# Spreading B with one bf16 product of three parts instead of an fp32 product, in a kernel whose scans run on VectorE

## The chip, the cores and the metric

The kernel runs on one core of a Trainium2 chip. Its time is the device time of one launch in microseconds (us). Before the change the median of three runs is 10359.18 us (10338.47 to 10376.03).

A core has a matrix engine (TensorE, "PE" in the profile, with its weight loads as "PEld"), VectorE ("DVE"), ScalarE ("ACT") and GpSimd ("POOL"). Each works through its own queue in order, and semaphores order the engines among themselves. The queue "SP" only issues DMAs here.

## The reference

The input is x of shape (4, 56, 56, 96), four images of 3136 tokens with 96 channels. Layers 0 and 1 are state-space layers with 192 inner channels and 16 states, each scanned in four directions; layers 2 and 3 are a linear attention and a quantised feed-forward net each. What matters here is the scan of layers 0 and 1, which is the same for each of the 4 images, 2 layers and 4 directions:

```python
xz = jnp.einsum('bld,kd->blk', seq, xw)
dt_raw = xz[..., :DT_RANK]
b_ssm = xz[..., DT_RANK:DT_RANK + D_STATE]
c_ssm = xz[..., DT_RANK + D_STATE:]
dt = jax.nn.softplus(jnp.einsum('blr,dr->bld', dt_raw, dtw) + dtb)
a = -jnp.exp(A_log)
d_a = jnp.exp(dt[..., None] * a)
d_b = dt[..., None] * b_ssm[:, :, None, :]

def step(h, inp):
    da_t, db_t, x_t, c_t = inp
    h = da_t * h + db_t * x_t[..., None]
    y_t = jnp.einsum('bds,bs->bd', h, c_t)
    return (h, y_t)
```

So for every token there is, per channel and state, a decay exp(dt * a), an input dt * u * B, the recurrence, a product with C, and a sum over the states. dt, B and C are linear in the sequence.

## The kernel before

**Chunks and rounds.** A sequence is cut into 7 chunks of 448 tokens. With 2 layers, 4 images and 4 directions that makes 224 chunks. A chunk has 8 rounds r = 0 to 7: two halves e of the 192 channels times four groups q of states. So there are 1792 rounds. One round holds 128 partitions (4 states times 32 channels) times 3 groups g of 448 tokens.

**What a round does.** In `begin` TensorE spreads B over the partitions: `spread_b` (L560 to L564) multiplies the tile `cf`, which holds C, B and the low-rank part of dt as rows of the chunk, with the 0/1 matrix `sel`, in fp32, into the single PSUM buffer `b`. VectorE multiplies `du` (dt times u, spread by DMA) with `b` into `v` for groups 0 and 1 (L645). Group 2 is made by GpSimd (L625), from a copy of B that came by DMA with C in `cb`; in the rounds listed in `OWN` or `OWN_TAIL` VectorE makes group 2 as well. `OWN_TAIL` holds for images 1 to 3 of layer 1, `OWN` for all others. ScalarE makes the decays `da` in PSUM (L617). VectorE then runs three scans (L670), GpSimd multiplies all three groups with C into `hc` (L680), and two rounds later `add_up` has TensorE sum over states into `y` with four products of 32 columns (L700). ScalarE copies `y` out (L707).

**Zero products.** Ahead of these four products `add_up` issues bf16 products of a zero matrix with `some`, the upper halves of fp32 words, which change nothing in `y` (L696). Their number is fixed when the program is built: as many as the round's other listed work falls short of `WARM`, divided by `FILL`. `self.work` counts what `spend` was told since the last `add_up`, times `PER_P`; neither B's product nor the four sums are in it.

**Preparing the next chunks.** During the 8 rounds of a chunk, `prepare` makes the next one ready: at r = 0 `rows` (ScalarE copies the projection from PSUM into `cf`), at r = 1 `step_sizes` (C and B to memory, first product for dt), at r = 2 `softplus` (ScalarE, with a change of its function table), at r = 3 and 4 `times_u` (GpSimd), then the spreading DMAs. `project_step` (L423) projects the chunk after that at r = 6 and 7, in fp32.

**The order of the work.** In the scans the order on each engine is the order of the program text. Beside the scans run lanes: the rest of the network for other images (norms, convolutions, projections), as generators that are resumed twice a round, at places "C" and "F", under budgets for ScalarE and TensorE. On TensorE the order of one round is: the lanes' products at "C", B's product for the next round, zero products and the four sums of two rounds ago, projections, the lanes' products at "F". A product that waits holds up all that stands behind it. Few lines carry the places that matter:

```python
ps = self.psum.tile([128, 512], F32, tag="b", name="b", bufs=1)[:, :CS]
self.nc.tensor.matmul(ps, self.sel[:, q], ch.cf, start=True, stop=True)
...
for _ in range(int(max(0.0, WARM - self.work) / FILL + 0.5)):
    nc.tensor.matmul(self.y[:C], self.zeros, self.some, start=False, stop=False)
```

After the scans the lanes that remain run alone, until the end.

Of the kernel before, what the change touches and what calls it, by code (L numbers as in the profile page):

```python
# [11 lines left out]
F32 = mybir.dt.float32  # L12
F16 = mybir.dt.float16
BF16 = mybir.dt.bfloat16
F8 = mybir.dt.float8e5
AF = mybir.ActivationFunctionType
ALU = mybir.AluOpType
# [5 lines left out]
C = 96  # L23
DI = 192
NS = 16
NE = 2
NG = 3
NQ = 4
# [4 lines left out]
CS = 448  # L33
# [2 lines left out]
RANK = (12, 6)  # L36
NW, LATE_NW = 13, 20
NWIN = 3
OWN = (3, 4)
OWN_TAIL = (3, 4)  # L40

SPARE = (1.2, 3.0)
# [3 lines left out]
DEPTH, LATE_DEPTH = 3, 6  # L46


WARM, FILL, PER_P = 1.5, 0.19, 0.58

ORDER = (((0, 0), (0, 1), (1, 0), (1, 1)), ((0, 1), (1, 0), (1, 1), (0, 0)))
WD = NE * 64 + NE * C + NE + NE * NQ * NG

# [29 lines left out]
def lay_out(i):  # L85
    i = {k: np.asarray(v) for k, v in i.items()}
    c96, c128, w96, w128, q96, q128 = Cols(C), Cols(128), Cols(C), Cols(128), Cols(C), Cols(128)
    p0, p1 = "L0_conv_", "L1_conv_"

    for n in ("norm_w", "norm_b", "norm2_w", "norm2_b", "ffn_b2"):  # L90
        c96.add("0" + n, i[p0 + n][:, None])
    for n in (
        "dw_b bn1_g bn1_b bn1_m bn1_v pw_b bn2_g bn2_b bn2_m bn2_v ln_g ln_b fus_b fus_ln_g fus_ln_b"
    ).split():
        c96.add("1" + n, i[p1 + n][:, None])
    c96.add("1dw_w", i[p1 + "dw_w"].reshape(C, 9))
    for l in "23":
        c96.add(l + "bq", i[f"L{l}_attn_bqkv"][:C, None])
        c96.add(l + "bff", i[f"L{l}_attn_bff"][:, None])
        c96.add(l + "b2", i[f"L{l}_ffn_b2"][:, None])  # L100
        c128.add(l + "b1", i[f"L{l}_ffn_b1"].reshape(3, 128).T)

    scan = (
        (i[p0 + "ssm_xw"], i[p0 + "ssm_dtw"], i[p0 + "ssm_dtb"], i[p0 + "ssm_Alog"], i[p0 + "ssm_D"]),
        (
            i[p1 + "x_proj_w"],
            i[p1 + "dt_w"],
            i[p1 + "dt_b"],
            i[p1 + "A_logs"].reshape(4, DI, NS),
            i[p1 + "Ds"].reshape(4, DI),  # L110
        ),
    )
    wd = np.zeros((2, 4, 128, WD), np.float32)
    for l, (xw, dw, db, al, dd) in enumerate(scan):
        r = RANK[l]
        for k in range(4):
            t = xw[k].T
            m = np.zeros((128, NE, 64), np.float32)
            m[:C, :, :32] = np.concatenate([t[:, r + NS :], t[:, r : r + NS]], 1).reshape(NE, C, 32).swapaxes(0, 1)
            m[:C, :, 32 : 32 + r] = t[:, :r].reshape(NE, C, r).swapaxes(0, 1)  # L120
            wt = np.zeros((128, DI), np.float32)
            wt[32 : 32 + r] = dw[k].T
            bias = np.zeros((128, NE), np.float32)
            bias[:C] = db[k].reshape(NE, C).T
            a = al[k].reshape(NE, NG, 32, 4, NQ).transpose(3, 2, 0, 4, 1).reshape(128, -1)
            wd[l, k] = np.concatenate([m.reshape(128, -1), wt, bias, a], 1)
        c128.add(f"{l}D", dd.T.reshape(NE, C, 4).swapaxes(0, 1))
    c128.add("0dir", np.broadcast_to(i[p0 + "dir_w"], (128, 4)))
    c128.add("0b1", i[p0 + "ffn_b1"].reshape(3, 128).T)
    for n, v in (  # L130
        ("1conv_b", i[p1 + "conv_b"][:, None]),
        ("1conv_w", i[p1 + "conv_w"].reshape(DI, 9)),
        ("1g", i[p1 + "out_norm_g"][:, None]),
        ("1b", i[p1 + "out_norm_b"][:, None]),
    ):
        c128.add(n + "a", v[:128])
        c128.add(n + "b", v[128:])

    w96.add("0in", _in_blocks(i[p0 + "in_w"].T))
    w96.add("1in", _in_blocks(i[p1 + "in_proj_w"].T))  # L140
    w96.add("0w1", i[p0 + "ffn_w1"].T)
    w96.add("1pw", i[p1 + "pw_w"])
    f = i[p1 + "fus_w"].T
    w96.add("1fa", f[:C])
    w96.add("1fb", f[C:])
    w96.add("1out", i[p1 + "out_proj_w"])
    w = i[p0 + "out_w"].T
    w128.add("0outa", w[:128])
    w128.add("0outb", w[128:])
    w128.add("0w2", i[p0 + "ffn_w2"].T.reshape(3, 128, C).transpose(1, 0, 2))  # L150
    for l in "23":
        w96.add(l + "qkv", i[f"L{l}_attn_Wqkv"])
        w96.add(l + "ff", i[f"L{l}_attn_Wff"])
        q96.add(l + "w1", i[f"L{l}_ffn_W1"].T)
        q128.add(l + "w2", i[f"L{l}_ffn_W2"].T.reshape(3, 128, C).transpose(1, 0, 2))
    bqkv = np.stack([i[f"L{l}_attn_bqkv"] for l in "23"])
    cols = {"c96": c96, "c128": c128, "w96": w96, "w128": w128, "q96": q96, "q128": q128}
    arrays = {"x": np.ascontiguousarray(i["x"]).reshape(NB, L, C), "bqkv": bqkv, "wd": wd}
    arrays.update({k: v.array() for k, v in cols.items()})
    return arrays, {k: v.at for k, v in cols.items()}  # L160


class Net:
# [81 lines left out]
    def setup(self):  # L245
        nc, tc, const = self.nc, self.tc, self.const
        par = self.par
        self.tiles = {}
        for g in ("c96", "c128", "w128"):
            t = const.tile(list(self.aps[g].shape), F32, name=g)  # L250
# [43 lines left out]
        m = const.tile([128, 1], F32, name="wmax")  # L294
# [29 lines left out]
        for n, bias in (("bn1", "1dw_b"), ("bn2", "1pw_b")):  # L324
            s = const.tile([C, 1], F32, name=n + "s")
            t = const.tile([C, 1], F32, name=n + "t")
# [13 lines left out]
        self.b2q = const.tile([C, 2], F32, name="b2q")  # L340
        with tc.tile_pool(name="stage", bufs=1) as st:

            self.sel = const.tile([64, NQ, 128], F32, name="sel")
            for q in range(NQ):
                nc.vector.tensor_copy(
                    self.sel[:, q].rearrange("p (s d) -> p s d", s=4),
                    self.ident[:64, NS + q : NS + q + 13 : 4].unsqueeze(2).to_broadcast([64, 4, 32]),
                )
            self.some = self.upper(self.tiles["w128"][:, :CS])
            self.zeros = const.tile([128, C], BF16, name="zeros")  # L350
# [1 line left out]
            t = st.tile([C, 2, 3, 128], F32, name="q96")  # L352
# [66 lines left out]
    def project_step(self, ch, e):  # L419

        if e == 0:
            ch.ps = self.pp()[:64]
        self.nc.tensor.matmul(  # L423
            ch.ps.rearrange("p (a b) -> p a b", b=HS), ch.par.wx[:, e],
            self.in_order(self.U[e], ch.orient, ch.c * CS, CS), start=e == 0, stop=e == NE - 1,
        )

    def parameters(self, ch):

        nc, sp = self.nc, self.sp  # L430
        if ch.step == 0:
            self.p = p = Step()
            wd = sp.tile([128, WD], F32, name="wd")
            nc.sync.dma_start(wd, self.aps["wd"][ch.l, ch.k])
            a = NE * 64
            p.wx = wd[:C, :a].rearrange("p (e m) -> p e m", e=NE)
            p.wt = wd[:, a : a + NE * C]
            a += NE * C
            p.dtb = wd[:C, a : a + NE]
            p.alog = wd[:, a + NE :]  # L440
            p.na = sp.tile([128, NE, NQ, NG], F32, name="na")
            p.carry = sp.tile([128, NE, NQ, NG], F32, name="carry")
        ch.par = self.p
# [10 lines left out]
    def rows(self, ch):  # L454
        nc, sp, p = self.nc, self.sp, ch.par
        if ch.step == 0:
            na = p.na.rearrange("p e q g -> p (e q g)")
            nc.scalar.activation(na, p.alog, AF.Exp)
            nc.scalar.mul(na, na, -1.0)
        ch.cf = sp.tile([64, CS], F32, name="cf")  # L460
        if ch.l == 0:
            nc.scalar.activation(ch.cf, ch.ps, AF.Copy, scale=self.cscale[:64, ch.k : ch.k + 1])
        else:
            nc.scalar.copy(ch.cf, ch.ps)

# [56 lines left out]
    def prepare(self, ch, follow, r):  # L522

        if r == 0:
            self.spread(ch.du, ch.dud[1], "du")
            self.spread(ch.dt, ch.dtd[1], "dt")
            self.fetch(ch, 3)
        if follow is None:
            return
        if r == 0:  # L530
            self.rows(follow)
        elif r == 1:
            self.step_sizes(follow)
        elif r == 2:
            self.softplus(follow)
        elif r == 3:
            self.times_u(follow, 0)
            for e in range(NE):
                self.park(follow.dtd, follow.dtc[e])
        elif r == 4:  # L540
            self.times_u(follow, 1)
            self.park(follow.dud, follow.duc[0])
            self.spread(follow.dt, follow.dtd[0], "dt")
        elif r == 5:
            self.park(follow.dud, follow.duc[1])
            self.spread(follow.du, follow.dud[0], "du")
        if r > 4:
            self.fetch(follow, r - 5)
# [11 lines left out]
    def spread_b(self, ch, q):  # L560

        ps = self.psum.tile([128, 512], F32, tag="b", name="b", bufs=1)[:, :CS]
        self.nc.tensor.matmul(ps, self.sel[:, q], ch.cf, start=True, stop=True)  # L563
        return ps  # L564

    def upper(self, x):

        return x.bitcast(BF16).rearrange("p (t h) -> p t h", h=2)[:, :, 1]

    def scans(self):  # L570

# [700 lines left out]
```

## Time and profile before

| What | Value |
|---|---|
| Median of three runs | 10359.18 us |
| The profiled execution | 10376.03 us, span 10373.7 us |
| First and last scan | start at 119.3 us and 10002.7 us from the span's start |
| Mean granted TensorE clock | 0.829 |
| VectorE busy | 7858.5 us, 76% of the span |
| GpSimd busy | 7561.5 us, 73% |
| ScalarE busy | 6150.6 us, 59% |
| DMA | 136 GB/s over the span |

The time of the profiled execution is its span and 2.3 us around it; it is the slowest of the three runs, 0.16% over their median. The scans fill 97% of it. A busy TensorE isn't TensorE at its peak: the end of a product is modelled, and its tail overlaps with the next. The granted clock is the share of full speed that TensorE had.

### The profile page before, as it was taken

Reading aid. Unit: us, or ns where it says so; the run is one execution under the profiler, and the core shown is the slowest. Engines: PE = TensorE matmul, PEld = TensorE weight load, DVE = VectorE, ACT = ScalarE, POOL = GpSimd, SP = SyncE. Lnnn points to the kernel's source line nnn. Section 1 sums busy time; section 2 is a strip of 40 time slices with the busy share of each in tenths; the row PEclk is TensorE's granted clock in tenths of the full one; section 3 lists DMA queues with packets and bytes.
Section 4 is the critical chain, followed back from the end, with each engine's and each line's share of the span. In section 5 each row is a group of like instructions: output and inputs, shape, how many; then the busy total and the mean of one; then the engine's idle time right before and its main releaser. Section 6 shows DMA issues by size and latency. Waiting matters only on the chain. (4 is left out here: it accounts for less than half of the span.)

```text
span 10373.7 us, 122887 instructions
## 1 busy us (share of the span) xinstructions
PE 9476.3 (91%) x34929; PEld 3165.4 (31%) x34929; DVE 7858.5 (76%) x10056; ACT 6150.6 (59%) x12259; POOL 7561.5 (73%) x4012
## 2 busy tenths in 40 slices
PE   8999988999899989999899899998999999998997
PEld 3222222222222222222222233322333223332345
DVE  5887977888787987788777976878767777776851
ACT  5666666666666666666566654566545656455645
POOL 5776877878777887788776976768767677676841
PEclk8887988988888988899788987878777778786886
DMA  5665665657565665566555764546645456554631
GB/s 144 154 160 130 168 147 135 144 138 170 140 150 132 157 159 133 142 148 171 129 138 128 164 150 116 125 119 150 146 111 121 119 139 154 121 124 106 152 83 43
DMA packets 951345, 1415.93 MB, mean 136 GB/s; under 512 B 176578, under 2 KB 943812, under 8 KB 949796
## 3 DMA queue, kind: packets, MB, share of 16 engines
q1 hardware_dynamic: 949888, 1406.27, 56.3%
q8 instruction: 274, 4.49, 0.2%
q14 instruction: 411, 3.37, 0.1%
q10 hardware_dynamic: 772, 1.80, 0.1%
HBM read 1139.32 MB, written 268.14 MB: 136 GB/s over the span
## 5 line engine op out<-in xcount | busy, mean ns | idle before, releaser
L680 POOL TENSOR_TENSOR hc<-v,cb 128x1344 f32<-128x1344 f32 x1792 | 5157.6, 2879 | 1781.4 <-DVE v L670 1089.9
L670 DVE TENSOR_TENSOR_SCAN v<-da,v 128x449 f32<-128x449 f32 (+1 forms) x5376 | 5489.6, 1072 | 261.8 <-ACT da L617 151.9
L617 ACT ACTIVATE da<-dt,na 128x448 f32<-128x448 f32 x5376 | 3387.0, 635 | 2096.9 <-DVE v L670 2058.7
L645 DVE TENSOR_TENSOR v<-du,b 128x448 f32<-128x448 f32 x4032 | 2280.8, 612 | 1832.5 <-PE b L563 1544.0
L563 PE MATMUL b<-cf,sel 64*128 64x448 f32 x3584 | 2134.4, 680 | 160.9 <-DVE v L645 160.6
L700 PE MATMUL y<-hc,four 128*32 128x448 f32 x14336 | 2054.8, 650 | 0.0
L625 POOL TENSOR_TENSOR v<-du,cb 128x448 f32<-128x448 f32 x1344 | 1528.7, 1137 | 50.5 <-DMA cb<-cd 43.9
L696 PE MATMUL y<-w,zeros 128*96 128x448 bf16 x4795 | 1294.4, 407 | 0.0
L563 PEld LDWEIGHTS b<-cf,sel 64*128 64x128 f32 x3584 | 612.1, 210 | 1361.2 <-issue 466.7
L696 PEld LDWEIGHTS <-zeros 128*96 128x96 bf16 x4795 | 584.6, 134 | 992.5 <-issue 801.1
L707 ACT COPY Y<-y 96x448 f32<-96x448 f32 x448 | 341.1, 761 | 908.3 <-PE y L700 907.9
L747 POOL TENSOR_TENSOR rs<-rs,power 112x4 f32<-112x4 f32 x252 | 254.2, 1009 | 852.7 <-ACT rs L746 465.9
L423 PE MATMUL pp<-U,wd 96*64 96x448 f32 x896 | 674.9, 842 | 4.5 <-DMA U<-u 4.5
L700 PEld LDWEIGHTS y<-hc,four 128*32 128x32 f32 x14336 | 302.2, 116 | 1223.9 <-issue 855.5
L827 PE MATMUL ps<-win,dg 64*64 64x220 f32 (+10 forms) x1962 | 585.4, 503 | 46.1 <-ACT dtc L488 42.8
L694 PE MATMUL y<-Y,ident 96*96 96x448 f32 x672 | 576.1, 948 | 5.6 <-ACT carry L674 3.8
L494 POOL TENSOR_TENSOR duc<-dtc,U 96x448 f32<-96x448 f32 x448 | 557.8, 1245 | 7.8 <-ACT dtc L488 7.8
L617 ACT ACT_TABLE_LOAD x385 | 494.0, 1283 | 14.6 <-DMA dt<-dd 7.8
L751 PE MATMUL ps<-ident,rs 112*96 112x112 f32 x1752 | 292.8, 328 | 117.5 <-POOL rs L747 58.4
L674 ACT COPY carry<-v 128x3 f32<-128x3 f32 x1536 | 295.0, 192 | 154.6 <-DVE v L670 150.2
L827 PEld LDWEIGHTS ps<-win,dg 64*64 64x64 f32 (+2 forms) x1962 | 240.3, 172 | 446.1 <-issue 349.1
L725 PE MATMUL ps<-w,cen 96*96 96x448 f32 x448 | 262.1, 681 | 110.3 <-ACT dtc L488 28.1
(411 smaller groups left out, 6293.3 us busy)
## 6 DMA issues: line engine op xcount, KB each, us to landing
cb<-cd SPq DMA_DIRECT2D x3584, 112.0 KB, 4.0
dt<-dd SPq DMA_DIRECT2D x1792, 168.0 KB, 4.3
du<-dd SPq DMA_DIRECT2D x1792, 168.0 KB, 3.9
dd<-dtc SPq DMA_DIRECT2D x448, 168.0 KB, 2.0
dd<-duc SPq DMA_DIRECT2D x448, 168.0 KB, 2.0
U<-u SPq DMA_DIRECT2D x112, 168.0 KB, 4.6
z<-w SPq DMA_DIRECT2D x56, 224.0 KB, 3.7
u<-w SPq DMA_DIRECT2D x56, 224.0 KB, 2.8
```

The costliest lines, as they stand in the source:

```text
L423: self.nc.tensor.matmul(ch.ps.rearrange("p (a b) -> p a b", b=HS), ch.par.wx[:, e], self.in_order(self.U[e], ch.orient, ch.c * CS, CS), st ...
L494: self.nc.gpsimd.tensor_tensor(du.rearrange("p (a b) -> p a b", b=HS), ch.dtc[e].rearrange("p (a b) -> p a b", b=HS), self.in_order(self.U ...
L563: self.nc.tensor.matmul(ps, self.sel[:, q], ch.cf, start=True, stop=True)
L617: nc.scalar.activation(da[g][:, TOKENS], ch.dt[e][:, g], AF.Exp, scale=ch.par.na[:, e, q, g : g + 1])
L625: nc.gpsimd.tensor_tensor(v[:, 2, TOKENS], ch.du[e][:, 2], ch.cb[q][:, 1], ALU.mult)
L645: nc.vector.tensor_tensor(v[:, g, TOKENS], ch.du[e][:, g], b, ALU.mult)
L670: nc.vector.tensor_tensor_scan(v[:, g, way], da[g][:, way], v[:, g, way], 0.0, ALU.mult, ALU.add)
L680: nc.gpsimd.tensor_tensor(hc, v[:, :, TOKENS], ch.cb[q][:, 0].unsqueeze(1).to_broadcast([128, NG, CS]), ALU.mult)
L694: nc.tensor.matmul(o, w, self.in_order(a, ch.orient, ch.c * CS, CS), start=True, stop=False)
L696: nc.tensor.matmul(self.y[:C], self.zeros, self.some, start=False, stop=False)
L700: nc.tensor.matmul(self.y[32 * n : 32 * n + 32], self.four, hc[:, g], start=n == 3, stop=n == 3 or q == NQ - 1,)
L827: self.nc.tensor.matmul(o[:, a - r0 : e - r0, x0:x1], diag[:, tap], win[:, a + dy - lo : e + dy - lo, x0 + dx : x1 + dx], start=n == 0, st ...
```

## The change

The program's three text changes are these.

1. B is spread by one bf16 product. The projection's weights get 128 columns in place of 64: columns 64 to 95 and 96 to 127 repeat the C and B columns. `cf` so has 128 rows, with three copies of C and B. `split`, called at r = 1 and r = 2 for the next chunk, has GpSimd subtract from the second and third copy their upper bf16 halves, then from the third again. The upper halves of the three copies are then the high, middle and low part of each number, and `sel`, now a bf16 matrix of 128 rows, adds the three.
2. `OWN` is (3, 4, 6) in place of (3, 4): in layer 0 and in image 0 of layer 1, VectorE makes group 2 in round 6 as well.
3. `WARM` is 1.9 in place of 1.5: two more zero products in a round that has less listed work than that.

```diff
-OWN = (3, 4)
+OWN = (3, 4, 6)
 OWN_TAIL = (3, 4)
...
-WARM, FILL, PER_P = 1.5, 0.19, 0.58
+WARM, FILL, PER_P = 1.9, 0.19, 0.58
...
-WD = NE * 64 + NE * C + NE + NE * NQ * NG
+WD = NE * 128 + NE * C + NE + NE * NQ * NG
...
-            m = np.zeros((128, NE, 64), np.float32)
...
+            m = np.zeros((128, NE, 2, 64), np.float32)
...
+            m[:, :, 1, :32] = m[:, :, 1, 32:] = m[:, :, 0, :32]
...
-            self.sel = const.tile([64, NQ, 128], F32, name="sel")
+            self.sel = const.tile([128, NQ, 128], BF16, name="sel")
+            parts = st.tile([128, 128], F32, name="parts")
+            nc.vector.tensor_tensor(parts[:, :32], self.ident[:, 64:96], self.ident[:, 96:], ALU.add)
+            nc.vector.tensor_tensor(parts[:, :32], parts[:, :32], self.ident[:, :32], ALU.add)
...
-            ch.ps = self.pp()[:64]
+            ch.ps = self.pp()
...
-        ch.cf = sp.tile([64, CS], F32, name="cf")
+        ch.cf = sp.tile([128, CS], F32, name="cf")
...
         elif r == 1:
             self.step_sizes(follow)
+            self.split(follow, 0)
         elif r == 2:
             self.softplus(follow)
+            self.split(follow, 1)
...
-        self.nc.tensor.matmul(ps, self.sel[:, q], ch.cf, start=True, stop=True)
+        self.nc.tensor.matmul(ps, self.sel[:, q], self.upper(ch.cf), start=True, stop=True)
         return ps
 
     def upper(self, x):
 
         return x.bitcast(BF16).rearrange("p (t h) -> p t h", h=2)[:, :, 1]
+
+    def split(self, ch, n):
+        x = ch.cf[64 + 32 * n :]
+        self.nc.gpsimd.tensor_tensor(x, x, self.upper(x), ALU.subtract)
```

More of the change, by code (lines that the diff above doesn't have):

```diff
@@ L117, in lay_out @@
             t = xw[k].T
-            m = np.zeros((128, NE, 64), np.float32)
-            m[:C, :, :32] = np.concatenate([t[:, r + NS :], t[:, r : r + NS]], 1).reshape(NE, C, 32).swapaxes(0, 1)
-            m[:C, :, 32 : 32 + r] = t[:, :r].reshape(NE, C, r).swapaxes(0, 1)
+            m = np.zeros((128, NE, 2, 64), np.float32)
+            m[:C, :, 0, :32] = np.concatenate([t[:, r + NS :], t[:, r : r + NS]], 1).reshape(NE, C, 32).swapaxes(0, 1)
+            m[:C, :, 0, 32 : 32 + r] = t[:, :r].reshape(NE, C, r).swapaxes(0, 1)
+            m[:, :, 1, :32] = m[:, :, 1, 32:] = m[:, :, 0, :32]
             wt = np.zeros((128, DI), np.float32)
@@ L346, in setup @@
                     self.sel[:, q].rearrange("p (s d) -> p s d", s=4),
-                    self.ident[:64, NS + q : NS + q + 13 : 4].unsqueeze(2).to_broadcast([64, 4, 32]),
+                    parts[:, NS + q : NS + q + 13 : 4].unsqueeze(2).to_broadcast([128, 4, 32]),
                 )
@@ L434, in parameters @@
             nc.sync.dma_start(wd, self.aps["wd"][ch.l, ch.k])
-            a = NE * 64
+            a = NE * 128
             p.wx = wd[:C, :a].rearrange("p (e m) -> p e m", e=NE)
@@ L459, in rows @@
             nc.scalar.mul(na, na, -1.0)
-        ch.cf = sp.tile([64, CS], F32, name="cf")
+        ch.cf = sp.tile([128, CS], F32, name="cf")
         if ch.l == 0:
-            nc.scalar.activation(ch.cf, ch.ps, AF.Copy, scale=self.cscale[:64, ch.k : ch.k + 1])
+            nc.scalar.activation(ch.cf, ch.ps, AF.Copy, scale=self.cscale[:, ch.k : ch.k + 1])
         else:
```

## The prediction

> **What bounds the kernel now.** I read the page's groups first, then the waits, then stretches of the trace with the granted clock beside the number of scans, then the timeline of a quiet stretch. The groups:
>
> ```profile
> L680 POOL TENSOR_TENSOR hc<-v,cb 128x1344 f32<-128x1344 f32 x1792 | 5157.6, 2879 | 1781.4 <-DVE v L670 1089.9
> L670 DVE TENSOR_TENSOR_SCAN v<-da,v 128x449 f32<-128x449 f32 (+1 forms) x5376 | 5489.6, 1072 | 261.8 <-ACT da L617 151.9
> L645 DVE TENSOR_TENSOR v<-du,b 128x448 f32<-128x448 f32 x4032 | 2280.8, 612 | 1832.5 <-PE b L563 1544.0
> L563 PE MATMUL b<-cf,sel 64*128 64x448 f32 x3584 | 2134.4, 680 | 160.9 <-DVE v L645 160.6
> L625 POOL TENSOR_TENSOR v<-du,cb 128x448 f32<-128x448 f32 x1344 | 1528.7, 1137 | 50.5 <-DMA cb<-cd 43.9
> L696 PE MATMUL y<-w,zeros 128*96 128x448 bf16 x4795 | 1294.4, 407 | 0.0
> ```
>
> Columns: instructions, busy us and mean ns, idle us before them and what ended it. VectorE's largest wait is for B: 1544 us. From the waits (total, times, longest):
>
> ```profile
> DVE v L645 <- PE b L563: 1544.0, 773, 6.7
> PEld b L563 <- DVE v L670: 465.0, 486, 2.6
> PEld y L700 <- POOL hc L680: 135.9, 182, 1.6
> ```
>
> So in 773 of 1792 rounds VectorE waits 2.0 us for B; in the other 57% B is early. What tells the two apart? Stretches of 500 us, scans only (busy us, count, granted clock, DMA share, GB/s), and below them all engines in 101 and 59 us:
>
> ```profile
> 5500.00:6000.00 500.00, 312.42 (x307) 0.92 0.64 151
> 8000.00:8500.00 500.00, 255.40 (x249) 0.72 0.52 123
> ...
> 5830.70:5932.10 101.40, 90.13 (x408) 29.51 (x408) 99.71 (x127) 65.73 (x142) 94.70 (x49) 1.00 0.71 168
> 8957.20:9016.00 58.80, 56.90 (x166) 19.55 (x165) 36.64 (x49) 25.36 (x49) 38.75 (x21) 0.63 0.45 105
> ```
>
> The order is PE, PEld, DVE, ACT, POOL, then clock. At clock 1.00 three chunks take 101.4 us, VectorE is busy 99.71 of it and GpSimd 94.70: VectorE bounds, GpSimd is 5% behind, and B costs nothing. At 0.63 one chunk takes 58.8 us, PE is busy 56.90, VectorE only 36.64: TensorE bounds. The kernel changes between the two with the clock. A quiet round at full clock:
>
> ```profile
> 5864.66 1.02 PE L563 MATMUL b<-cf,sel 64*128 64x448 f32 x2 [0.29 <-DVE v L645]
> 5865.61 1.78 PE L696 MATMUL y<-w,zeros 128*96 128x448 bf16 x8
> 5867.32 0.96 PE L700 MATMUL y<-hc,four 128*32 128x448 f32 x8
> ...
> 5002.06 1.86 PE L563 MATMUL b<-cf,sel 64*128 64x448 f32 x2
> ```
>
> B holds TensorE for 0.95 us (5864.66 to 5865.61), a zero product 0.214 us (8 in 1.71), the sums 0.89. The last line is B at half clock: 1.86 us.
>
> [...] Here fp32 B holds TensorE 0.95 us against 0.214 for a bf16 product as wide, 4.4 times. [...] I price the new subtraction, which has two inputs, by L625[...].
>
> **The change, part by part.** Against the profiled execution (10374 us of span, 2 us around it, 0.16% over the median).
>
> *B's product.* 1792 fp32 products (3584 instructions) become 1792 bf16 ones, with the moving operand at every second half-word, as the zero products have it. Row L696 prices them: 0.36 us alone at full clock, 0.61 at half (its shortest and longest records, 357 and 609 ns). So VectorE gets B 0.66 us (1.02 - 0.36) or 1.25 us (1.86 - 0.61) sooner after its start. Each of the 773 waits is 2.0 us on average, yet some are shorter than the saving: I take 0.8 us each, -620 us. Nothing below -773 x 1.25 = -966 except by clearing more backlog; not above -773 x 0.4 = -309, if the short waits are many. Where VectorE doesn't wait for B the saving is worth nothing.
>
> *The zero products.* Counting lines of the built programs, they go from 4795 to 7084. 641 rounds, those with much lane work, have none before or after; the other 1151 gain two (a few gain one). Two cost 0.43 us at full clock, 0.75 at half. They stand on TensorE before the next B. In a quiet round at full clock they are covered (TensorE waits for VectorE before B: the 465 us above). At half clock they are not: 773 waits, 64% of them behind such a round, some 0.4 us: +200, between 0 (cover everywhere) and +370 (0.75 x 64% x 773). B and zeros together: -420.
>
> *Group 2 in round 6.* 140 chunks (112 of layer 0, 28 of layer 1) move one product from GpSimd (1137 ns) to VectorE (612 ns): +86 us of VectorE, hidden in the 43% of rounds where it waits for B: +50 (0 to 86).
>
> *GpSimd's subtractions.* 448 instructions of 448 columns with two inputs. GpSimd's cost follows columns here, not partitions (L494 on 96 and L625 on 128: 1245 and 1137 ns), so 1.13 us each for 64 or 32 partitions: +506 us, less 140 x 1.137 = -159: +347 us of GpSimd. They stand in rounds 1 and 2, ahead of `hc`, behind which the sums wait on TensorE. They wait only for `cf`, made a round earlier. GpSimd's idle time ahead of `hc` is 1781 us, one microsecond a round, so most is covered on average. In the full-clock stretch it isn't: 94.7 + 6 x 1.13 - 3 x 1.137 = 98.1 us of GpSimd against 99.7 + 3 x 0.61 = 101.5 of VectorE, in chunks that now take 101.4. In images 1 to 3 of layer 1, where `OWN_TAIL` keeps GpSimd's share, it would be 101.5 against 99.7. I put a third on the path: +115 (0 to +347).
>
> *The clock.* This decides. In a quiet round TensorE's work before its next wait falls from 3.55 us (0.95 + 1.71 + 0.89) to 3.24 (0.21 + 2.14 + 0.89); in the 641 loaded rounds 0.74 us go with nothing in their place. Mean: (1151 x 0.31 + 641 x 0.74) / 1792 = 0.46 us a round, out of some 4.5. TensorE then sits idle more, most where it is held by ScalarE or GpSimd[...]. Over nineteen stretches of 500 us (the first left out) the fit is 3.6 scans per 0.01 of clock, of 271: 1.3%. That holds the lanes' own load too, and at half clock the new round is lighter; I take half, 0.7% or 70 us per 0.01. The trace can't price the clock's fall: at least 0 (`WARM` does its work), at most 0.10 (the 10% of TensorE's work that goes). I take 0.06, to 0.77: +420.
>
> *Free edits.* Projection to 128 columns: as many moving columns, only the weight load is longer, under running products; worth 136 ns more on 448 x 2 loads at worst. ScalarE's copy to `cf`: same columns, 629 and 526 ns, not more with partitions. `wd` is 512 bytes a partition longer in 32 DMAs issued a chunk ahead. `sel` is made in the setup: two small VectorE instructions, about 1 us. SP's queue has as many DMAs as before (3584 for `cb`, 1792 each for `dt` and `du`).
>
> Sum: -420 + 50 + 115 + 420 = +165; 10374 + 165 = 10539, less 0.16% for the median of runs: 10520.
>
> **The rivals.**
> - *Faster, because the clock holds.* Mechanism: TensorE's saved 0.66 to 1.25 us end VectorE's wait for B, and the two added zeros keep the clock at 0.82 or more. For it: in loaded rounds TensorE is late anyway, so less work need not mean idle time. Against it: 0.46 us less work a round, where clock losses already set the pace. Sum without the clock's term: -420 + 50 + 115 = -255, 10374 - 255 = 10119, 10100 for the median. It decides above a clock of 0.829 - 255/70/100 = 0.793: above, the kernel is faster. Chance 0.27.
> - *A wash*: clock near 0.79, within 0.3% (31 us, about what three runs with a spread of 0.36% can tell from no change). Chance 0.08.
> - *GpSimd takes VectorE's place as the bound.* All +347 on the path, `hc` late, TensorE held at the sums, clock at 0.76 (+480): -420 + 50 + 347 + 480 = +457, 10815 for the median. For it: 5% of slack at full clock. Against it: GpSimd idles 1781 us ahead of `hc`. Chance 0.17.
> - *The split doesn't do what it says*, say because the subtractions wait for the DMA of `cf` or B's product waits for them each round. The built program shows them waiting for ScalarE and GpSimd alone, a round or more before B needs them: under 0.01.
>
> **How the numbers follow.** The forecast, slower at 10520, has 0.48. Slower by over 0.3%: 0.48 + 0.17 = 0.65; faster 0.27; same 0.08. The range runs from 10050, below the middle of the faster case, with about 0.11 under it, to 10900, with 0.07 over it: the spread of the clock's term (0 to +700), of B (-966 to -309) and of GpSimd. The forecast alone would have 10390 to 10750.
>
> **What would show it.** Right: wait of L645 for B from 1544 to 900 us or less; B's product near 0.4 us mean; mean clock near 0.77; the wait of the sums for GpSimd up from 136 us; GpSimd busy near 7910, VectorE near 7945. Wrong: a clock of 0.80 or more with the wait for B halved (the faster rival), or a clock of 0.77 with a shorter span (70 us per 0.01 too dear). If the wait for B stays near 1500 us, B was never late by its own length but by what stands before it.

## The result, and the profile after

The changed kernel takes 9195.01 us, the median of four runs (9183.7 to 9210.96), against 10361.14 us for the kernel before, the median of four runs too: a ratio of 0.8877, 95% interval 0.8855 to 0.89. The forecast was slower, at 10520 us; the measured time is 11% faster and lies below the whole range, and below the faster rival's 10100 too. The profiled execution has a span of 9209.2 us and a mean granted clock of 0.887, where the kernel before had 10373.7 us and 0.829.

The page's engines and groups after, with the same columns as before (instructions, busy us and mean ns, idle us and what ended it). The lines of the program have moved: the scans now stand at L684, the products with B at L659, B's product at L569.

```profile
PE 7868.1 (85%) x35426; PEld 3036.5 (33%) x35426; DVE 7881.9 (86%) x10198; ACT 6148.3 (67%) x12259; POOL 7838.3 (85%) x4320
...
L684 DVE TENSOR_TENSOR_SCAN v<-da,v 128x449 f32<-128x449 f32 (+1 forms) x5376 | 5484.4, 1072 | 244.6 <-ACT da L631 111.0
L694 POOL TENSOR_TENSOR hc<-v,cb 128x1344 f32<-128x1344 f32 x1792 | 5168.0, 2885 | 573.5 <-DVE v L684 257.2
L659 DVE TENSOR_TENSOR v<-du,b 128x448 f32<-128x448 f32 x4172 | 2342.3, 609 | 663.0 <-PE b L569 532.4
L710 PE MATMUL y<-w,zeros 128*96 128x448 bf16 x7084 | 1716.6, 380 | 0.0
L569 PE MATMUL b<-cf,sel 128*128 128x448 bf16 x1792 | 708.3, 395 | 350.9 <-DVE v L659 350.1
...
L582 POOL TENSOR_TENSOR cf<-cf 64x448 f32<-64x448 f32 x448 | 417.7, 932 | 38.1 <-ACT cf L466 3.0
```

The scans cost what they did. VectorE's wait for B is down from 1544.0 to 532.4 us, GpSimd's idle time ahead of `hc` from 1781.4 to 573.5. From the waits (us in total, times, longest):

```profile
DVE v L659 <- PE b L569: 532.4, 369, 6.5
...
PEld y L714 <- POOL hc L694: 115.7, 221, 1.6
```

VectorE now waits for B in 369 rounds in place of 773, 1.4 us each in place of 2.0. The sums wait no longer for GpSimd than before (135.9 us then). Of stretches of 500 us, scans alone, the one with the highest clock and the one with the lowest (busy us, count, granted clock, DMA share, GB/s):

```profile
5000.00:5500.00 500.00, 330.40 (x324) 0.94 0.69 164
...
8000.00:8500.00 500.00, 288.27 (x282) 0.83 0.60 141
```

The stretch with the lowest clock, 8000 to 8500 us in both kernels, now holds 282 scans; before it held 249. And the quiet round, TensorE's timeline (start, length):

```profile
5208.12 0.36 PE L569 MATMUL b<-cf,sel 128*128 128x448 bf16 x1 [0.79 <-DVE v L659]
5208.32 2.14 PE L710 MATMUL y<-w,zeros 128*96 128x448 bf16 x10
5210.39 0.96 PE L714 MATMUL y<-hc,four 128*32 128x448 f32 x8
```

B holds TensorE for 0.20 us and ten zero products for 2.07, as the prediction had priced them (0.21 and 2.14). TensorE's work in a quiet round did fall. The clock rose all the same.

### The profile page after: what moved, and what is told of

Read it like the earlier page. It is cut to its first block, busy times and chain, and to the rows that moved or that the text cites. A ratio compares the mean times of both kernels' runs of the same rounds, so it can differ in the third digit from the quotient of the medians.

```text
span 9209.2 us, 124390 instructions
## 1 busy us (share of the span) xinstructions
PE 7868.1 (85%) x35426; PEld 3036.5 (33%) x35426; DVE 7881.9 (86%) x10198; ACT 6148.3 (67%) x12259; POOL 7838.3 (85%) x4320
## 5 line engine op out<-in xcount | busy, mean ns | idle before, releaser
L684 DVE TENSOR_TENSOR_SCAN v<-da,v 128x449 f32<-128x449 f32 (+1 forms) x5376 | 5484.4, 1072 | 244.6 <-ACT da L631 111.0
L694 POOL TENSOR_TENSOR hc<-v,cb 128x1344 f32<-128x1344 f32 x1792 | 5168.0, 2885 | 573.5 <-DVE v L684 257.2
L659 DVE TENSOR_TENSOR v<-du,b 128x448 f32<-128x448 f32 x4172 | 2342.3, 609 | 663.0 <-PE b L569 532.4
L714 PE MATMUL y<-hc,four 128*32 128x448 f32 x14336 | 1913.8, 609 | 0.0
L710 PE MATMUL y<-w,zeros 128*96 128x448 bf16 x7084 | 1716.6, 380 | 0.0
L639 POOL TENSOR_TENSOR v<-du,cb 128x448 f32<-128x448 f32 x1204 | 1373.7, 1141 | 79.0 <-DMA cb<-cd 41.6
L710 PEld LDWEIGHTS <-zeros 128*96 128x96 bf16 x7084 | 918.5, 130 | 1049.4 <-issue 639.9
L569 PE MATMUL b<-cf,sel 128*128 128x448 bf16 x1792 | 708.3, 395 | 350.9 <-DVE v L659 350.1
L427 PE MATMUL pp<-U,wd 96*128 96x448 f32 x896 | 674.5, 840 | 14.3 <-DMA U<-u 14.3
L708 PE MATMUL y<-Y,ident 96*96 96x448 f32 x672 | 543.4, 898 | 11.4 <-ACT carry L688 8.9
L582 POOL TENSOR_TENSOR cf<-cf 64x448 f32<-64x448 f32 x448 | 417.7, 932 | 38.1 <-ACT cf L466 3.0
L569 PEld LDWEIGHTS <-sel 128*128 128x128 bf16 x1792 | 195.4, 109 | 741.4 <-issue 737.9
```

What stands on the lines that cost most here:

```text
L427: self.nc.tensor.matmul(ch.ps.rearrange("p (a b) -> p a b", b=HS), ch.par.wx[:, e], self.in_order(self.U[e], ch.orient, ch.c * CS, CS), st ...
L569: self.nc.tensor.matmul(ps, self.sel[:, q], self.upper(ch.cf), start=True, stop=True)
L639: nc.gpsimd.tensor_tensor(v[:, 2, TOKENS], ch.du[e][:, 2], ch.cb[q][:, 1], ALU.mult)
L659: nc.vector.tensor_tensor(v[:, g, TOKENS], ch.du[e][:, g], b, ALU.mult)
L684: nc.vector.tensor_tensor_scan(v[:, g, way], da[g][:, way], v[:, g, way], 0.0, ALU.mult, ALU.add)
L694: nc.gpsimd.tensor_tensor(hc, v[:, :, TOKENS], ch.cb[q][:, 0].unsqueeze(1).to_broadcast([128, NG, CS]), ALU.mult)
```

## Where a half-clock stretch doesn't end

The trace's clock records of the kernel before hold 316 stretches at half clock, 11.25 us long on average. The changed kernel has as many, 316, of 6.57 us. So in one run the clock is not lost less often; it comes back sooner. Three of the long stretches of the kernel before, all engines (PE, PEld, DVE, ACT, POOL, then clock):

```profile
6908.90:6953.30 44.40, 43.80 (x108) 12.07 (x107) 26.53 (x35) 24.50 (x53) 26.19 (x15) 0.50 0.40 98
8110.40:8154.80 44.40, 43.79 (x107) 12.13 (x107) 25.87 (x35) 22.79 (x48) 25.65 (x14) 0.50 0.38 90
8212.80:8257.20 44.40, 43.81 (x107) 11.79 (x106) 26.24 (x35) 24.34 (x53) 26.05 (x15) 0.50 0.40 95
```

TensorE is busy for 43.8 of 44.4 us in each, by the trace's modelled ends, and stays at half clock throughout. Being busy doesn't bring the clock back here. What runs in the first of them (the numbers after the line and operation: tile, rows*columns of the array, moving operand):

```profile
6925.39 1.72 PE L700 MATMUL y<-hc,four 128*32 128x448 f32 x8
6927.04 1.80 PE L475 MATMUL pp<-cf,wd 6*96 6x448 f32 x2
6928.78 1.81 PE L1088 MATMUL ps<-w,wq 96*96 96x448 f32 x2
6930.52 1.86 PE L563 MATMUL b<-cf,sel 64*128 64x448 f32 x2
```

Products that feed 6, 64 or 96 of the 128 rows stand beside the full ones, and one follows the other without a gap. B's product was one of 64 rows; after the change it is one of 128. That is an effect of the change that neither its words nor my prediction named. The experiments were to tell it from the shorter time on TensorE, the kind of number, and the zero products.

A count over the whole trace of the kernel before points the same way. All its half-clock stretches but the last are whole multiples of 3.413 us. Cut them into pieces of that length, and count each product from its start to the next one's start, or to its own end. In 862 pieces TensorE is then busy for 99% or more, and only 310 of these end with the return to full clock: none of the 337 in which the products fed less than 0.75 of the 128 rows, averaged over the piece; 46 of the 231 between 0.75 and 0.85; 264 of the 294 above. A count only sorts what happened; the experiments vary the rows.

## The experiments

Each was timed against the kernel before on its own chip; its median there was 10332.05 us for the first four below, 10349.33 for the two that follow and for the two under "No zero products" and "Group 2 of round 6", and 10371.58 for the other four. Ratios carry 95% intervals.

**All of the change but B's product.**

```diff
-OWN = (3, 4)
+OWN = (3, 4, 6)
-WARM, FILL, PER_P = 1.5, 0.19, 0.58
+WARM, FILL, PER_P = 1.9, 0.19, 0.58
```

(on the kernel before)

> The kernel before with WARM 1.9 and OWN (3, 4, 6): all of the change but B's product and the subtractions. Theory 'occupancy' (the gain is the TensorE time that B no longer takes, and the clock follows because the backlog clears sooner): no gain, 10350 to 10700 us, clock 0.80 to 0.84, wait for B 1500 us or more. Theory 'zeros' (the two added zero products raise the clock, and the rest follows): 9300 to 9900 us, clock 0.87 or more.

Measured: 10495.69 us, ratio 1.015 (1.0118 to 1.0181), clock 0.858. More zero products and the moved group together raise the clock by 0.029, and the kernel gets 1.5% slower. VectorE waits for B no less than before (1544.0 us then):

```profile
DVE v L645 <- PE b L563: 1553.8, 809, 7.7
```

So these two are not the gain, and a higher mean clock is not by itself time.

**The change with WARM back at 1.5.**

```diff
-WARM, FILL, PER_P = 1.9, 0.19, 0.58
+WARM, FILL, PER_P = 1.5, 0.19, 0.58
```

> The changed kernel with WARM back at 1.5. Occupancy: 9100 to 9400 us, as the change (fewer zero products, clock 0.86 to 0.89). Zeros: the clock falls back to 0.83 or less and the time to 9700 us or more.

Measured: 9162.29 us, ratio 0.8867 (0.8831 to 0.8902), clock 0.86. The interval holds the change's 0.8877: nothing told apart, at a clock lower by 0.027.

**The change without the subtractions.**

```diff
-            self.split(follow, 0)
+            pass
...
-            self.split(follow, 1)
+            pass
```

> The changed kernel without GpSimd's 448 subtractions; B is then three times its high part, so the output is another one. Prices the subtractions: if a third of GpSimd's added time lies on the path, 9050 to 9120 us; if GpSimd bounds now, 8750 to 8950 us; if they are covered, 9180 to 9210 us.

Measured: 9162.44 us, ratio 0.8865 (0.884 to 0.8889), clock 0.889. The intervals overlap: by the medians the subtractions cost 33 us, which is not told apart from nothing. GpSimd isn't the bound.

**B's bf16 product four times.**

```diff
-        self.nc.tensor.matmul(ps, self.sel[:, q], self.upper(ch.cf), start=True, stop=True)
+        for _ in range(4):
+            self.nc.tensor.matmul(ps, self.sel[:, q], self.upper(ch.cf), start=True, stop=True)
```

> The changed kernel with B's bf16 product issued four times into the same buffer[...]. Occupancy: most of the gain goes, 9900 to 10500 us, clock 0.82 to 0.85. Rival 'kind' (fp32 products hold the granted clock low, bf16 ones don't): 9300 to 9600 us with a clock of 0.87 or more, since the kind stays bf16.

Measured: 9651.82 us, ratio 0.9343 (0.9322 to 0.9364), clock 0.935. Neither theory: the passes cost 457 us over the change, so time on TensorE counts, but with TensorE busy in B's products for 1837.0 us (at clock 0.935), against 2134.4 in the fp32 ones before (at 0.829), the kernel is still 680 us faster than before. The kind of number fits, and so do the rows: 128 here, 64 in fp32.

**The same over 64 rows.**

```diff
-            self.nc.tensor.matmul(ps, self.sel[:, q], self.upper(ch.cf), start=True, stop=True)
+            self.nc.tensor.matmul(ps, self.sel[:64, q], self.upper(ch.cf)[:64], start=True, stop=True)
```

(in the loop of four)

> As the four bf16 products of B, but each over 64 rows of cf in place of 128, as the fp32 product has them; the middle and low parts of B are left out, so the output is another one. Theory 'rows' ([...]64 rows keep it low): clock 0.83 to 0.88 and 9900 us or more, against 0.935 and 9652 us with 128 rows. Theory 'gaps' (fp32 keeps the clock low by the weight load between its halves[...]): unchanged, 9600 to 9700 us at 0.92 to 0.94.

Measured, ten runs: 10400.49 us, ratio 1.0044 (1.002 to 1.0068), clock 0.861. Still bf16, as many products, but half the rows: the 680 us are gone. The waits of the two, 128 rows and then 64:

```profile
DVE v L660 <- PE b L570: 927.5, 574, 6.7
```

```profile
DVE v L660 <- PE b L570: 1438.7, 751, 7.1
```

With 64 rows the wait for B is nearly that of the kernel before.

**fp32 over 128 rows**, with WARM 1.9 and OWN (3, 4, 6). The projection has the change's 128 columns, there are no subtractions, and rows 64 to 127 of `sel` are zero:

```diff
-            self.sel = const.tile([64, NQ, 128], F32, name="sel")
+            self.sel = const.tile([128, NQ, 128], F32, name="sel")
...
-        ch.cf = sp.tile([64, CS], F32, name="cf")
+        ch.cf = sp.tile([128, CS], F32, name="cf")
```

> The fp32 kernel with WARM 1.9 and OWN (3, 4, 6), its product over 128 rows (the upper 64 rows of sel are zero, the projection has the change's 128 columns); layer 1 uses layer 0's skip factors, so the output is another one. Rows: the clock rises to 0.91 or more from 0.858 and the time falls below 10000 us from 10496. Gaps: no change, 10400 to 10600 us at 0.84 to 0.87.

Measured: 9655.7 us, ratio 0.9336 (0.9306 to 0.9365), clock 0.933. It is 840 us under the same kernel with 64 rows (medians, against 10495.69), and not told apart from four bf16 products over 128 rows (0.9343), which has the subtractions besides. So the gain hangs on the rows and not on the kind. Over 64 rows the kinds are not quite equal: 1.015 in fp32 (the first experiment) against 1.0044 in bf16, with intervals apart; why is open. The wider projection, which comes with the 128 rows here, isn't the cause: the bf16 kernel over 64 rows has it too, and its clock is 0.861.

**The kernel before, with nothing but the rows.** The same edit with WARM 1.5 and OWN (3, 4); as there, the projection is the wider one and layer 1 has no skip factors of its own.

> The kernel before (WARM 1.5, OWN (3, 4), fp32 product) with nothing changed but the rows of B's product: 128, the upper 64 rows of sel zero, the projection with 128 columns; layer 1 uses layer 0's skip factors. Theory 'rows': what 64 more rows bring doesn't hang on the rest of the change: 9400 to 9650 us, clock 0.90 or more. If the rows help only together with the added zero products: above 9900 us.

Measured: 9436.48 us, ratio 0.9102 (0.9079 to 0.9125), clock 0.924. Its rows of the page, and its wait for B:

```profile
PE 8267.8 (88%) x34929; PEld 3127.8 (33%) x34929; DVE 7824.8 (83%) x10054; ACT 6149.3 (65%) x12259; POOL 7553.1 (80%) x4012
...
PEclk8998999999999999999999999999899999998986
...
L565 PE MATMUL b<-cf,sel 128*128 128x448 f32 x3584 | 1895.8, 613 | 244.4 <-DVE v L655 242.0
```

```profile
DVE v L655 <- PE b L565: 850.3, 512, 7.1
```

As many instructions on TensorE as before (34929), 3584 of them B's in both, not one product fewer: yet the clock stands at 0.9 or more nearly throughout, and the wait for B falls from 1544.0 to 850.3 us. Its clock records hold 253 half-clock stretches of 5.67 us. This one property brings 935 us to the kernel before. The whole change brings 1166, but 935 is not the rows' share of it, as the next experiment shows.

**The change with its one product over 64 rows.**

```diff
-        self.nc.tensor.matmul(ps, self.sel[:, q], self.upper(ch.cf), start=True, stop=True)
+        self.nc.tensor.matmul(ps, self.sel[:64, q], self.upper(ch.cf)[:64], start=True, stop=True)
```

> The changed kernel with its one bf16 product over the first 64 rows alone; the middle and low parts of B are left out. Rows: even one pass in a round of 64 rows delays the return to full clock: clock 0.80 to 0.87, 9300 to 9700 us, a loss of a fifth to a half of what it was with four passes (749 us). If rows matter only where four passes hold TensorE: 9190 to 9230 us.

Measured: 9566.97 us, ratio 0.9233 (0.9206 to 0.9261), clock 0.853. Even with a single pass a round, feeding 64 rows in place of 128 costs 372 us, half of what it costs with four. Its wait for B, where the change has 532.4 us:

```profile
DVE v L659 <- PE b L569: 761.1, 540, 6.3
```

Four of these kernels now differ in B's product alone, all bf16, with WARM 1.9 and OWN (3, 4, 6) (medians in us, and the clock):

| B's product | 64 rows | 128 rows |
|---|---|---|
| four passes | 10400.49, 0.861 | 9651.82, 0.935 |
| one pass | 9566.97, 0.853 | 9195.01, 0.887 |

The added rows bring 749 us with four passes and 372 with one. Three passes fewer bring 833 us with 64 rows and 457 with 128. Each is worth less where the other is already there, so the 1166 us can't be split into a share of each. And in both columns fewer passes lower the clock, while the time falls.

**No zero products.**

```diff
-WARM, FILL, PER_P = 1.9, 0.19, 0.58
+WARM, FILL, PER_P = 0.0, 0.19, 0.58
```

> The changed kernel with no zero products at all (WARM 0). Occupancy theory: the clock falls to 0.75 to 0.82, but half-clock rounds are short; 9250 to 9700 us. If the zero products carry the gain: above 10000 us.

Measured: 9230.42 us, ratio 0.8926 (0.8907 to 0.8945), clock 0.73. Its clock by slices of the page, and its waits:

```profile
PEclk7777677776787677866778668776877767876786
```

```profile
PE b L569 <- DVE v L659: 806.7, 477, 14.0
DVE v L659 <- PE b L569: 648.0, 428, 7.3
```

The clock falls by 0.157, more than twice the fall of my forecast, and costs 35 us by the medians. TensorE waits for VectorE 806.7 us ahead of B: it has time to be slow. In this kernel the zero products, now 7084, are worth 0.4%.

**Group 2 of round 6 back on GpSimd.**

```diff
-OWN = (3, 4, 6)
+OWN = (3, 4)
```

> The changed kernel with OWN (3, 4): GpSimd makes group 2 in round 6 again, 140 products. If VectorE bounds: 40 to 80 us faster than the change's 9195. If GpSimd bounds: 50 to 160 us slower.

Measured: 9184.33 us, ratio 0.888 (0.8864 to 0.8896). No difference from the change, which neither expectation had.

**Two tries at a faster one.** First WARM 1.2 with OWN (3, 4):

> The changed kernel with WARM 1.2 and OWN (3, 4), which the runs so far point to as a faster one: 9120 to 9170 us, clock 0.83 to 0.86.

Measured: 9172.84 us, ratio 0.8846 (0.8821 to 0.8871), clock 0.822: just above the expected range, and not told apart from the change. Then more rows for the products that make dt, the change otherwise:

```diff
-        rows = slice(32, 32 + RANK[ch.l])
+        rows = slice(0, 64)
```

> The changed kernel with the products for dt (448 of them) over 64 rows of cf in place of 12 or 6, the added rows of the weights being zero. Rows: the clock rises above 0.887, to 0.89 to 0.91, and the time falls by 20 to 100 us. If the rows of these products don't count: 9180 to 9210 us.

Measured: 9186.12 us, ratio 0.8862 (0.8839 to 0.8884), clock 0.895. The clock moves as the rows theory has it, by 0.008; the time is not told apart from the change's. No version beats the change by more than the intervals.

## Why the prediction was wrong

**The step that failed** is "The clock": "TensorE then sits idle more, most where it is held by ScalarE or GpSimd". That idle time would cost clock, and how much, was my estimate: +420 us on a fall to 0.77; the clock rose to 0.887. The work did fall as counted. Two things in the step were wrong.

First, I took the time that TensorE is busy as what holds and restores its clock. The same fp32 products over 128 rows in place of 64 lifted it from 0.829 to 0.924. Less work did lower the clock, as the step had it: from four passes to one it fell from 0.935 to 0.887 with 128 rows and from 0.861 to 0.853 with 64. The rows outweighed that. The profile before had the sign of it: TensorE busy 56.90 of 58.80 us at clock 0.63 was read as "TensorE bounds"; why the clock stayed low in so busy a stretch I did not ask. The three stretches above stayed at half clock for 44.4 us. And the row for B printed 64*128 where the diff made `sel` 128 rows. I had dismissed the wider projection as a free edit; it is what makes those rows.

Second, a fall of 0.06 was priced at 420 us. Where fewer passes lowered the clock, the time fell too, by 457 and 833 us; and with the zero products gone a fall of 0.157 cost 35 us. Had the rows stayed at 64, the forecast would have failed too: with one pass over 64 rows the kernel takes 9566.97 us, already below the whole range and below the faster rival; the rows are 372 of the 1325 us between the forecast and the result. The sign of being wrong that the prediction named first, a clock of 0.80 or more with the wait for B halved, is what came.

**The price of the clock.** 70 us per 0.01 came from stretches in which a low clock and much lane work went together. The measured prices: 35 us for 0.157 without zero products, a loss of 164 us at a gain of 0.029 in the first experiment, 935 us for 0.095 with the rows. The mean clock has no single price. What goes with the time is VectorE's wait for B: 648.0 us at clock 0.73 without zero products, 1544.0 us at 0.829 in the kernel before, 1553.8 us at 0.858 in the first experiment.

**B and the zeros**, -420 us at an unchanged clock: the right sign, too small. Three passes fewer bring 457 us with 128 rows and 833 with 64, where I had put 620 us on B's product. The zeros' +200 us isn't to be seen behind a bf16 product (9162 us with WARM 1.5, 9195 with 1.9). Ahead of an fp32 product over 64 rows, WARM 1.9 and OWN together cost 164 us. The wait for B fell by 1012 us, past my bound of 966, which allowed for more only "by clearing more backlog"; the shorter half-clock stretches fit that.

**GpSimd**: +347 us of work forecast, 277 measured (7561.5 to 7838.3). A subtraction takes 932 ns, not the 1130 that I took from L625. The cost in time is 33 us by the medians, not told apart from nothing, where I had put 115. VectorE's busy time rose by 23 us in all, and the moved product can't be told from none, where I had put 50.

**The faster rival** had the right side, and its mechanism holds where the rows stay at 64: from four passes to one the clock stays at 0.853 and the time falls by 833 us. It put 255 us on this and had no reason for a rise of the clock. Its claim that the kernel is faster above a clock of 0.793 is void too: without zero products it is faster at 0.73.

## What to carry to other kernels

Where TensorE is busy without a break and still at half clock, as in 43.8 of 44.4 us here, look at how many rows its products feed, not only at how long they take. Padding a product's contraction to 128 rows with zero weights brought 9% here (935 of 10371.58 us), its own cost included, where that product was in fp32; feeding 128 rows in place of 64 brought 4% (372 of 9566.97 us) where it was one bf16 product. Don't price a mean clock: ask whether TensorE is late or early where the clock is low.

## What the runs showed of the hardware

- In the kernel before, TensorE stayed at half clock for 44.4 us while busy for 43.8 of them. Of the 316 half-clock stretches of its trace, all but the last were whole multiples of 3.413 us long.
- 128 rows in place of 64 in one of the round's products took the mean clock from 0.829 to 0.924 (fp32, weights of the added rows zero), from 0.858 to 0.933 (the same with more zero products), from 0.861 to 0.935 (four bf16 products) and from 0.853 to 0.887 (one bf16 product). Numbers of rows between 64 and 128 were not run for this product, and no run varies the columns alone.
- An fp32 product over 128 rows and four bf16 products of the same size gave times not told apart (ratios 0.9336 and 0.9343); over 64 rows fp32 was slower (1.015 and 1.0044).
- A GpSimd subtraction of 448 columns, in place, with one operand as upper half-words, took 932 ns for 64 and for 32 rows alike (931 to 936 in all 448 records of the changed kernel); the fp32 product of 448 columns with two operands took 1137 ns (mean of L625 in the kernel before).
